# Joining the score matmuls of a tile into one planned step, with a new set of durations and priorities for a planned kernel

## The chip, the cores and the metric

The kernel runs on one core of one Trainium2 chip. The metric is the time of one execution on the device, in microseconds. Three runs of the kernel before gave 4202.29, 4206.68 and 4212.64 us; the median is 4206.68 us.

## The reference, cut to what matters

The input is sixteen sequences of 256 tokens with 128 features each, all in f32. Four blocks follow each other, and after each the sum of its input and output is normalised:

```python
x = layernorm(x + linear_attention(x))     # 4 heads of 32
x = layernorm(x + experts(x))              # 8 experts, 2 chosen, one shared
x = layernorm(x + feature_attention(x))    # 16 heads of 64, causal, softmax features
x = layernorm(x + stack(x))                # six layers
```

The six-layer stack holds the code whose matmuls are joined. Each layer is

```python
x = attention(shift_tokens(x)) + x   # 16 heads of 64, window of 32 and the 32 keys before it
x = feed_forward(shift_tokens(x)) + x   # layernorm, 128 -> 2 x 341, a * gelu(gate), 341 -> 128
```

In the attention, queries and keys are brought to length one, scaled, rotated, and multiplied for each head and each window of 32 queries with 64 keys. A masked softmax over those 64 keys weighs the values.

## The kernel before, in words

The kernel has two stages, and each has its own planner (`class Plan`). A stage is written as a set of steps. A step has an engine (`pe` is TensorE, `act` ScalarE, `dve` VectorE, `pool` GpSimd, `sp` the queue that starts DMAs), an assumed duration in us, a Python function that emits its instructions, the steps it must follow, the buffers that it takes or uses, and a rank. `Plan.run` goes through an assumed time on the host: whenever an engine is free, it takes from the ready steps the one of the lowest rank whose buffers are free, calls its function, and so writes the instructions down in that order. After a step's assumed duration and a lag per engine (`LAG`) its followers become ready. What comes out is a fixed order per engine; on the chip each engine runs its list in order and waits on semaphores. So durations, lags and ranks cost nothing by themselves on the chip: they only choose the order and the buffers. The ranks come from the position of the work (tile number), a table `due`, and the dictionary given to `Plan`, which adds a number to all steps of one function.

The first stage (the front) runs the three blocks ahead of the stack for eight units of two sequences. Its steps are `linear`, `experts`, `causal` and `part`.

The second stage runs six layers of eight units, 48 units in all. For each sequence, and in it for each tile of 128 tokens (two per sequence):

- `projections` (matmuls L1091) makes queries and keys in a `pair` buffer of PSUM; there are four `pair` buffers for the whole stage. L1112 squares them, L1098 and L1105 multiply with the rotary tables, L1115 adds, L1118 sums the squares.
- `turned` transposes them (L1165) and L1171 copies them out to `qT` and `kT`.
- `attention`: `scores` (L1239) multiplies queries and keys in small tiles, 64 rows by 32 columns, 64 matmuls per tile of tokens, into one `pair` buffer. `mask` (L1247) adds the mask, `top` (L1261) takes maxima, `exps` (L1273) exponentiates, `total` and `divide` (L1280, L1284) normalise, `turn` (L1288) transposes 32x32 blocks, and `mix` (L1298, tiles of 32 rows by 128 columns) multiplies with the inputs into two `pair` buffers, which L1307 copies out.
- `output` (L1346) applies the joined value and output weights for a sequence; `windows` (L1215) transposes its input.
- `feed_forward` does a unit of two sequences: L1372, L249, then six matmul steps `inner` (L1407) with gelu (L1414) and gating (L1420), and `outer` (L1427).

In the kernel before, `scores` is four steps per tile, each of 16 matmuls, one after the other:

```python
for g in range(4):
    sc.append(step("pe", 0.38, partial(scores, g), [..., *sc[-1:]],
                   [] if g else [pS], ..., rank + due["scores"], count=64))
```

The `pair` buffer is taken by the first of them and held until the mask has read the last. `count` is the number of instructions that the step issues on TensorE: an f32 matmul is two weight loads and two matmul records, so 16 matmuls are 64. The planner uses it in `_dense`, which holds back a step with a count over 32 as long as it and the steps before it would bring more than `BLOCK` = 256 counted instructions within `SPAN` = 3.6 us of assumed time.

Of the kernel before, what the change touches and what calls it, by code (L numbers as in the profile page):

```python
# [48 lines left out]
class Step:  # L49


    def __init__(self, eng, work, fn, after, takes, uses, rank, table, count):
        self.eng, self.work, self.fn, self.rank = eng, work, fn, rank
        self.count = count
        self.takes, self.uses, self.table = takes, uses, table
        self.next, self.wait = [], 0
        for b in (*takes, *uses):
            b.left += 1
        for s in after:
            s.next.append(self)  # L60
            self.wait += 1


class Plan:
# [6 lines left out]
    BLOCK, SPAN = 256, 3.6  # L71
# [7 lines left out]
    def step(self, eng, work, fn, after=(), takes=(), uses=(), rank=0, table=None, count=0):  # L79
# [3 lines left out]
        s = Step(eng, work, fn, after, takes, uses, rank, table, count)  # L83
# [3 lines left out]
    def run(self):  # L87
# [10 lines left out]
        now, table, opened = 0.0, None, {}  # L98
        past = []
        left = len(self.steps)  # L100
        self.log = []
        self.unique = 0
        while left:
            moved = True
            while moved:
                moved = False
                for eng, heap in ready.items():
                    if at[eng] > now or not heap:
                        continue
                    back, got, kept = [], None, ()  # L110
                    while heap and len(back) < 64:
                        item = heapq.heappop(heap)
                        s = item[2]
                        if s.table and opened and s.table not in opened:
                            back.append(item)
                            continue
                        if s.count > 32 and self._dense(s, now, past, events):
                            back.append(item)
                            continue
                        kinds = [b.kind for b in s.takes]  # L120
                        if all(self._fits(kinds, k) for k in set(kinds)) and not any(k in kept for k in kinds):
                            got = s
# [8 lines left out]
                        back.append(item)  # L131
                    for item in back:
# [5 lines left out]
                    work = got.work  # L138
                    if got.table:
# [15 lines left out]
                    if got.count:  # L155
                        past.append((now, got.count))
                        del past[:-40]
# [18 lines left out]

    def _dense(self, s, now, past, events):

        room = self.BLOCK - s.count
        for t, c in reversed(past):  # L180
            room -= c
            if room < 0:
                wait = t + self.SPAN - s.work
                if wait > now + 1e-6:
                    self.unique -= 1
                    heapq.heappush(events, (wait, self.unique, None))
                    return True
                return False
        return False
# [10 lines left out]
def tile_kernel(ctx: ExitStack, tc: tile.TileContext, a: dict, out: bass.AP):  # L200
# [84 lines left out]
    def join(step, kinds, i, lay, after, rank):  # L285
# [45 lines left out]
        for g in range(2):  # L331
            b, v, pt, pz = (Buf(k) for k in kinds)
            ld = step("sp", 2.0, partial(fetch, g, b), after, [b], [], rank)
            tn = step("pe", 0.59, partial(turn, b, pt), [ld], [pt], [b], rank, count=8)
            cp = step("act", 0.59, partial(turned_out, v, pt), [tn], [v], [pt], rank)
            pm = step("pe", 1.09, partial(product, b, v, pz), [cp], [pz], [b, v], rank, count=32)
            lay.joined.append(step("act", 0.97, partial(put, g, pz), [pm], [], [pz], rank))
# [10 lines left out]
    with ExitStack() as st:  # L348
# [5 lines left out]
        def several(pl, n, shape, name):  # L354
# [17 lines left out]
            "part.turn": 1.5,  # L372
            "experts.gated": -4,
            "experts.outer": -0.5,
            "part.divide": -2,
            "part.diagonal": -6,
            "linear.peak": -0.5,
            "experts.hidden": 1.5,
            "part.values": 1.5,
            "part.ratio": -3,  # L380
            "experts.inner": 1.0,
            "part.below": -2,
            "experts.gates": -3.0,
            "part.weigh": 2,
            "experts.turn": -4.5,
            "linear.turn": 2,
            "linear.result": 3,
            "linear.context": -2,
            "norm.stats": 1.5,
            "causal.final": 3,  # L390
            "join.product": 3,
            "part.product": -4,
            "linear.feature": -1.5,
        })
        due = {
# [57 lines left out]
        def norm(name, get, put, after, takes, uses, rank):  # L453
# [24 lines left out]
            s1 = step("dve", 2.0, stats, after, [], uses, rank)  # L478
            s2 = step("pool", 1.05, root, [s1], rank=rank)
            return step("dve", 1.4, normal, [s2], takes, uses, rank)  # L480
# [8 lines left out]
        def linear(u, before):  # L489
# [15 lines left out]
            t1 = step("pe", 0.5, partial(turn, xn, pt), [n1], [pt], [xn], rank, count=8)  # L505
# [4 lines left out]
            af = step("act", 0.78, affine, [t1, wla], [xnT], [pt], rank)  # L510
# [4 lines left out]
            kk = step("pe", 0.9, partial(feature, 1, pk), [af], [pk], [xnT], rank, count=4)  # L515
# [7 lines left out]
            mk = step("dve", 0.7, peak, [kk], [], [pk], rank)  # L523
# [10 lines left out]
            ex = step("act", 1.35, exps, [mk], [ek], [pk], rank, ("exp", 0))  # L534
            qq = step("pe", 0.9, partial(feature, 0, pq), [af], [pq], [xnT], rank, count=4)
            qc = copied(qT, None, pq, 512, [qq], [qT], [], rank, 0.59)
# [8 lines left out]
            vv = step("pe", 0.92, values, [af], [pv], [xnT], rank, count=16)  # L545
            vc = copied(v4, None, pv, 512, [vv], [v4], [], rank, 0.59)
            t2 = step("pe", 0.5, partial(turn, ek, pz), [ex], [pz], [ek], rank, count=8)
# [1136 lines left out]
```

## Time and profile before

| what | value |
| --- | --- |
| median of three runs | 4206.68 us |
| span of the profiled execution | 4210.5 us |
| busy share: TensorE, VectorE, ScalarE, GpSimd | 95%, 83%, 75%, 64% |
| granted TensorE clock, mean | 0.989 |
| second stage: from its first projection to the end | 1097.5 to 4210.5 us |
| one unit of it, from one output step to the next but one | 62.76 us (2068.36 to 2131.12) |
| TensorE's instruction records | 43728 matmuls, 43728 weight loads |

The profiled execution's own time stands beside the runs as its span, 4210.5 us: 3.8 us above the median, and inside what the three runs cover. "Busy" counts the time in which an engine has an instruction in it. Matmuls are pipelined, and an end in the profile is modelled, so what one step costs TensorE is read from the start of its first record to the start of the next step's first record. PE is TensorE's matmuls, PEld its weight loads, DVE VectorE, ACT ScalarE, POOL GpSimd.

### The profile page before, as it was taken

Reading aid. Unit: us, or ns where it says so; the run is one execution under the profiler, and the core shown is the slowest. Engines: PE = TensorE matmul, PEld = TensorE weight load, DVE = VectorE, ACT = ScalarE, POOL = GpSimd, SP = SyncE. Lnnn points to the kernel's source line nnn. Section 1 sums busy time; section 2 is a strip of 40 time slices with the busy share of each in tenths; the row PEclk is TensorE's granted clock in tenths of the full one; section 3 lists DMA queues with packets and bytes.
Section 4 is the critical chain, followed back from the end, with each engine's and each line's share of the span. In section 5 each row is a group of like instructions: output and inputs, shape, how many; then the busy total and the mean of one; then the engine's idle time right before and its main releaser. Section 6 shows DMA issues by size and latency. Waiting matters only on the chain.

```text
span 4210.5 us, 104604 instructions
## 1 busy us (share of the span) xinstructions
PE 4018.2 (95%) x43728; PEld 2659.0 (63%) x43728; DVE 3500.1 (83%) x5169; ACT 3177.9 (75%) x6138; POOL 2695.5 (64%) x2881
## 2 busy tenths in 40 slices
PE   8999999999789999999999999999999999999998
PEld 6777877877545565565565565565565565565555
DVE  6888888877688888888888888888888888888885
ACT  6666666675477887877887877887887877888885
POOL 2555455555567676676677677676767667767762
PEclk9999999999899999999999999999999999999999
DMA  3000000000000000000000000000000000000000
GB/s 91 4 6 4 6 1 4 4 4 3 20 2 2 12 13 2 7 12 2 13 2 7 12 2 13 2 7 12 2 13 2 7 12 2 2 2 7 9 12 19
DMA packets 30836, 37.03 MB, mean 9 GB/s; under 512 B 5406, under 2 KB 24348, under 8 KB 29596
## 3 DMA queue, kind: packets, MB, share of 16 engines
q1 hardware_dynamic: 30364, 30.35, 2.4%
q8 instruction: 343, 5.62, 0.6%
q14 instruction: 129, 1.06, 0.1%
HBM read 26.15 MB, written 4.19 MB: 7 GB/s over the span
## 4 chain that ended last, share of the span: by engine, by line
PE 41%; DVE 32%; ACT 12%; POOL 11%; issue 4%; SPq 0%; DMA 0%; ACTq 0%; POOLq 0%; DVEq 0%
DVE d_t L1105 8%; PE pp L1346 7%; DVE d_t L1098 7%; ACT d_sq L1112 5%; PE pp L1091 4%; PE pp L1165 3%; PE pp L1298 3%; ACT d_e L1273 3%; PE pp L1427 3%; DVE d_ss L1118 3%; POOL d_t L1115 3%; DVE d_eT L1288 2%; DVE d_e L1247 2%; PE pb L665 2%; DVE d_m L1261 2%
## 5 line engine op out<-in xcount | busy, mean ns | idle before, releaser
L1115 POOL TENSOR_TENSOR d_t<-d_t,d_t 128x1024 f32<-128x1024 f32 x384 | 905.7, 2364 | 483.6 <-DVE d_t L1098 444.2
L1273 ACT ACTIVATE d_e<-d_e,d_m,d_ny 128x64 f32<-128x64 f32 x3072 | 1063.6, 431 | 18.4 <-POOL d_m L1269 17.7
L1091 PE MATMUL pp<-d_wqkv,xs 128*128 128x512 f32 x1536 | 740.6, 611 | 19.6 <-ACT d_qT L1171 6.1
L1346 PE MATMUL pp<-d_zT,d_wvo 128*128 128x256 f32 x3072 | 684.6, 381 | 0.4 <-ACT d_qT L1171 0.2
L1346 PEld LDWEIGHTS pp<-d_zT,d_wvo 128*128 128x128 f32 x3072 | 577.5, 190 | 81.7 <-issue 2.4
L1112 ACT ACTIVATE d_sq<-pp 128x1024 f32<-128x1024 f32 x384 | 392.2, 1023 | 277.9 <-DVE d_t L1105 138.6
L1105 DVE TENSOR_TENSOR d_t<-pp,d_tab 128x1024 f32<-128x1024 f32 x384 | 467.2, 1217 | 121.2 <-ACT d_sq L1112 69.5
L1307 ACT COPY d_zT<-pp 128x1024 f32<-128x1024 f32 x384 | 369.3, 1012 | 231.2 <-PE pp L1298 231.2
L1098 DVE TENSOR_TENSOR d_t<-pp,d_tab 128x1024 f32<-128x1024 f32 x384 | 464.7, 1210 | 66.4 <-ACT d_sq L1112 64.4
L1284 POOL TENSOR_TENSOR d_e<-d_e,d_z 128x1024 f32<-128x1024 f32 x192 | 365.4, 1903 | 208.7 <-DVE d_z L1281 204.2
L1091 PEld LDWEIGHTS pp<-d_wqkv,xs 128*128 128x128 f32 x1536 | 276.0, 192 | 326.3 <-issue 239.6
L1118 DVE TENSOR_REDUCE d_ss<-d_sq 128x16 f32<-128x1024 f32 x384 | 461.6, 1202 | 7.8 <-ACT d_sq L1112 4.7
L1239 PEld LDWEIGHTS pp<-d_kT,d_qT 64*32 64x32 f32 x24576 | 234.2, 106 | 358.7 <-issue 307.8
L1165 PE MATMUL pp<-ident,d_t 128*128 128x128 f32 x3072 | 403.6, 277 | 36.3 <-ACT d_qT L1171 13.1
L1165 PEld LDWEIGHTS pp<-ident,d_t 128*128 128x128 f32 x3072 | 338.4, 142 | 151.8 <-POOL d_t L1161 49.1
L1298 PE MATMUL pp<-d_eT,d_xw 32*128 32x512 f32 x3072 | 408.3, 617 | 7.2 <-DVE d_e L1247 2.9
L855 POOL TENSOR_TENSOR c_e<-c_e,c_sm 128x1024 f32<-128x1024 f32 x128 | 248.7, 1950 | 178.2 <-DVE c_sm L851 125.0
L1161 POOL TENSOR_TENSOR d_t<-d_t,d_ny 128x1024 f32<-128x1024 f32 x192 | 361.5, 1903 | 0.0
L1407 PE MATMUL pp<-f_xn,d_w 128*128 128x512 f32 (+1 forms) x576 | 306.7, 622 | 49.5 <-ACT d_sq L1112 32.2
L1239 PE MATMUL pp<-d_kT,d_qT 64*32 64x64 f32 x24576 | 338.2, 223 | 6.6 <-issue 3.9
L1288 DVE STREAM_TRANSPOSE d_eT<-d_e 128x1024 f32<-128x1024 f32 x192 | 238.4, 1242 | 113.4 <-POOL d_e L1284 112.1
L1280 DVE TENSOR_REDUCE d_z<-d_e 128x16 f32<-128x1024 f32 x192 | 232.9, 1213 | 62.9 <-ACT d_e L1273 62.5
(186 smaller groups left out, 7176.3 us busy)
## 6 DMA issues: line engine op xcount, KB each, us to landing
d_wqkv<-L_ffn_Wqkv SPq DMA_DIRECT2D x6, 1024.0 KB
d_t<-L_ffn_Wqkv SPq DMA_DIRECT2D x10, 256.0 KB
d_t<-L_ffn_Wo SPq DMA_DIRECT2D x10, 256.0 KB, 3.4
a_xin<-L_attn_x SPq DMA_DIRECT2D x8, 256.0 KB, 2.8
keep<-bc_x SPq DMA_DIRECT2D x8, 256.0 KB, 2.0
d_t<-keep SPq DMA_DIRECT2D x8, 256.0 KB, 2.9
out<-d_t SPq DMA_DIRECT2D x8, 256.0 KB, 2.3
d_w<-L_ffn_W SPq DMA_DIRECT2D x6, 341.0 KB
```

The costliest lines, as they stand in the source:

```text
L1091: pe.matmul(pj.t[:, hf * 512 : (hf + 1) * 512], lhsT=xj, rhs=q.w["qkv"][:, c : c + 512], start=True, stop=True,)
L1098: dve.tensor_tensor(t1.t, heads(pj.t), bc(q.lay.tab[:, 0, t, cc], hs, 1), ALU.mult)
L1105: dve.tensor_tensor(t2.t.rearrange("p h (x d) -> p h x d", x=2), swapped(pj.t), bc(q.lay.tab[:, 1, t, cc].rearrange("p (x d) -> p x d", x= ...
L1112: act.activation(sq.t, heads(pj.t), AF.Square)
L1115: pool.tensor_tensor(t1.t, t1.t, t2.t, ALU.add)
L1118: dve.tensor_reduce(q.ss.t[:, t, qk, :], sq.t, AX.X, ALU.add)
L1165: pe.transpose(pz.t[:, c * P : (c + 1) * P], t1.t[:, 2 * c : 2 * c + 2, :].rearrange("p h d -> p (h d)"), ident,)
L1239: pe.matmul(pS.t[b * WIN : (b + 1) * WIN, s0 : s0 + 2 * WIN], lhsT=qT.t[r, c, b * WIN : (b + 1) * WIN], rhs=kT.t[r, c, k0 : k0 + 2 * WIN], ...
L1273: act.activation(each()[:, h, :], each()[:, h, :], AF.Exp, bias=o.m[:, h : h + 1], scale=norm_of(h),)
L1298: pe.matmul(ps[b // 2].t[:, (b % 2) * 512 : (b % 2 + 1) * 512], lhsT=q.xw.t[r, 2 * t + j, :], rhs=eT.t[r, j, :, :].rearrange("p h n -> p ( ...
L1307: act.copy(q.zT.t[:, b : b + 2, :, :].rearrange("p b h n -> p (b h n)"), pz.t)
L1346: pe.matmul(pr.t[:, :SEQ], lhsT=q.w["vo"][:, (h % 2) * 8 + h // 2, :], rhs=q.zT.t[:, :, h, :], start=(h == 0), stop=(h == HEADS - 1),)
```

## The change

The four score steps of a tile become one step of 64 matmuls, with an assumed duration of 1.07 us. `count`, `_dense`, `BLOCK` and `SPAN` are taken out. A step may have a `mode` instead; the score steps have the mode "scores" and the mix steps "mix", all others none. The planner adds `TURN` = 0.165 us of assumed time where TensorE's next step has another mode than the one before. With `STICK` = 1 (second stage only) it prefers a ready step of the mode at hand over one with another mode, if its rank is at most 1 higher. Nearly all assumed durations are set anew, mostly lower; so are the lags, and both dictionaries of priorities now name every step function, DMA steps included. The instructions of the steps themselves, the buffers and the work are the same.

```diff
-    BLOCK, SPAN = 256, 3.6
+    TURN, STICK = 0.165, 0.0
...
-                        if s.count > 32 and self._dense(s, now, past, events):
+                        if other and (s.rank > other[0] + self.STICK or s.mode != shape):
                             back.append(item)
+                            if s.rank > other[0] + self.STICK:
+                                break
                             continue
...
+                            if eng == "pe" and s.mode != shape and self.STICK and not other:
+                                other = item
+                                continue
...
+                    if eng == "pe" and got.mode != shape:
+                        work += self.TURN
+                        shape = got.mode
...
-    def _dense(self, s, now, past, events):
...
         plan = Plan(slots, {
-            "part.turn": 1.5,
-            "experts.gated": -4,
...
+            "tile_kernel.fetch_x": 9,
+            "tile_kernel.weights": 9,
...
         })
+        plan.LAG = {"pe": 0.16, "act": 0.2, "dve": 0.13, "pool": 0.61, "sp": 0.82}
...
         plan = Plan(slots, {
-            "projections.product": -9,
-            "attention.mix": -0.5,
...
+            "projections.product": -8.5,
+            "attention.scores": 2,
+            "attention.mix": -1,
+            "attention.put": -11,
...
         })
-        plan.LAG = {"pe": 0.27, "act": 0.2, "dve": 0.25, "pool": 0.2, "sp": 2.5}
+        plan.LAG = {"pe": 0.17, "act": 0.06, "dve": 0.02, "pool": 0.64, "sp": 3.08}
+        plan.STICK = 1
...
-                    "pe", 1.82, partial(product, qk, pj), [*q.ready, *q.loaded, q.gate(t)],
-                    [pj, t1], rank=rank + due["project"], count=8,
+                    "pe", 1.76, partial(product, qk, pj), [*q.ready, *q.loaded, q.gate(t)],
+                    [pj, t1], rank=rank + due["project"],
...
-            def scores(g):
-
-                for c in (2 * g, 2 * g + 1):
+            def scores():
+
+                for c in range(8):
                     for par in range(2):
...
-            sc = []
-            for g in range(4):
-                sc.append(
-                    step(
-                        "pe", 0.38, partial(scores, g), [o.done[0], *q.turned[: t + 1], *sc[-1:]],
-                        [] if g else [pS], [qT, kT] + ([pS] if g else []), rank + due["scores"],
-                        count=64,
-                    )
-                )
-            mk = step("dve", 1.19, mask, sc, [e], [pS], rank + due["mask"])
+            sc = [
+                step(
+                    "pe", 1.07, scores, [o.done[0], *q.turned[: t + 1]], [pS], [qT, kT],
+                    rank + due["scores"], mode="scores",
+                )
+            ]
+            mk = step("dve", 1.13, mask, sc, [e], [pS], rank + due["mask"])
...
-                "pe", 2.05, partial(mix, ps), [te, q.spread, *q.mixed], [*ps, *new],
-                [eT, q.xw] + ([] if new else [q.zT]), rank + due["mix"], count=32,
+                "pe", 1.93, partial(mix, ps), [te, q.spread, *q.mixed], [*ps, *new],
+                [eT, q.xw] + ([] if new else [q.zT]), rank + due["mix"], mode="mix",
```

The order that the planner now writes for a unit in the middle of the second stage can be read from the program without running it. TensorE has four score steps per unit, each as 64 matmuls in a row, and right behind each of them a mix step of another tile. The six `inner` steps stand together behind the third pair of these, apart from one projection after the first of them. In the whole program there are 191 places where TensorE comes to score matmuls from something else, where there were 637.

## The prediction

> **What bounds the kernel now.** I read the page first: shares of busy time, the queues, then the timeline of a unit in the middle of the second stage, and last the two places where TensorE stands still in the midst of score matmuls.
>
> ```profile
> PE 4018.2 (95%) x43728; PEld 2659.0 (63%) x43728; DVE 3500.1 (83%) x5169; ACT 3177.9 (75%) x6138; POOL 2695.5 (64%) x2881
> q8 instruction: 343, 5.62, 0.6%
> PE 41%; DVE 32%; ACT 12%; POOL 11%; issue 4%; SPq 0%; DMA 0%; ACTq 0%; POOLq 0%; DVEq 0%
> ```
>
> TensorE is the bound, with VectorE next. The second line is the fetching of instructions (packets, MB, share of the DMA engines): 343 packets for 2 x 43728 TensorE records, that is one packet of 16 KB for about 255 of them. Next, the windows view over one unit, and the timeline inside it:
>
> ```profile
> 2068.36:2131.12 62.76, 61.03 (x773) 37.09 (x772) 54.48 (x66) 50.76 (x97) 43.97 (x50) 1.00 0.06 20
> ```
>
> ```profile
> 2089.72 0.45 PE L1239 MATMUL pp<-d_kT,d_qT 64*32 64x64 f32 x32
> 2090.10 1.12 PE L1407 MATMUL pp<-f_xn,d_w 128*128 128x512 f32 x2
> 2091.16 0.45 PE L1239 MATMUL pp<-d_kT,d_qT 64*32 64x64 f32 x32
> 2091.54 1.12 PE L1407 MATMUL pp<-f_xn,d_w 128*128 128x512 f32 x2
> 2092.59 0.45 PE L1239 MATMUL pp<-d_kT,d_qT 64*32 64x64 f32 x32
> 2093.93 1.09 PE L1407 MATMUL pp<-f_xn,d_w 128*85 128x512 f32 x2 [0.88 <-ACT d_sq L1112]
> 2094.95 0.45 PE L1239 MATMUL pp<-d_kT,d_qT 64*32 64x64 f32 x32
> 2095.33 2.00 PE L1298 MATMUL pp<-d_eT,d_xw 32*128 32x512 f32 x16
> ```
>
> Order of the window's columns: length, then busy us of PE, PEld, DVE, ACT, POOL, clock, DMA share, GB/s. PE has work in 61.03 of 62.76 us at full clock, but "busy" hides loss: a group of 16 score matmuls costs 0.38 (start to next start), and an L1407 that is followed by one costs 1.05 (2090.10 to 2091.16) where it costs 0.86 before other work. This score tile holds one of the four PSUM buffers from 2089.72 to 2095.33.
>
> The unit counted step by step, at the shortest start-to-start of each kind: 8 projections x 1.72, 8 transposes x 0.87, 2 windows x 0.44, 4 mixes x 1.93, 2 outputs x 6.91, 6 inner x 0.86, outer 2.68, two turns x 0.44: 51.9 us. Scores: 13 single groups x 0.385 and one run of three, 1.20: 6.2. What the step ahead of a score group lasts longer, 14 times, from 0.06 (mix) and 0.09 (projection) to 0.19 (L1346, 7.10 for 6.91): 2.0 together, mean 0.143. That is 60.1; the other 2.6 us are waits, the largest 0.95, 0.67 and 0.58 us.
>
> **Scores joined.** In the fill of the stage four groups stand in one run:
>
> ```profile
> 1246.40 1.49 PE L1239 MATMUL pp<-d_kT,d_qT 64*32 64x64 f32 x128
> 1247.81 1.13 PE L1298 MATMUL pp<-d_eT,d_xw 32*128 32x512 f32 x4
> ```
>
> 64 matmuls take 1.42 us to the next start, and that is the new step with the new follower, a mix. Four per unit are 5.7 for 6.2: 0.52 x 48 units = 25 us saved. Entries fall from 637 to 191 by the two programs' orders: 446 x 0.143 = 64 us. All of it lies on TensorE, the path. Together **-89 us**.
>
> **The guard taken out.** `_dense` kept 256 counted instructions from following each other within 3.6 us. What it guarded against shows where its accounting failed:
>
> ```profile
> 1278.22 2.53 PE L1239 MATMUL pp<-d_kT,d_qT 64*32 64x64 f32 x219 [0.32 <-DVE d_t L1098]
> 1282.72 0.31 PE L1239 MATMUL pp<-d_kT,d_qT 64*32 64x64 f32 x5 [1.97 <-issue]
> ```
>
> Two tiles' scores ran at full rate and then TensorE stopped for 1.97 us with nothing to wait for but issue. An instruction packet starts at 1280.08; the next score matmul starts 2.6 us after that. A second stop, 1.14 us at 1159.37, has a packet at 1157.00, 2.4 us ahead. My reading: the packet for the page after next is asked for when a page of 256 begins, and a page that runs out sooner than that packet is usable stops TensorE. From the beginning of the page (256 instructions before the last one that ran) to the resumption I count 3.4 us at the first stop and 3.1 at the second; pages of the steady stage that lasted 3.16 to 3.20 us end without a stop. I take 3.2.
>
> A joined step is 256 instructions, a page in length; its fastest 256 take 1.1 to 1.3 us. It is hit only where its place in the pages is nearly aligned, so that fewer than some 20 instructions of other work (about 9 per us) fall into the same page. A unit has 1540 instructions plus a few waits, six pages and a little, so the place drifts slowly and comes by every offset. Laying the program's TensorE instructions into pages of 256, each priced as above, gives 37 pages of 343 below 3.2 us, short of it by 37.5 us in sum (31 us at 3.0, 45 at 3.4). The same count on the kernel before gives 12 pages and 5.6 us. So **+32 us** (26 to 40); below nothing is excluded, since more dense pages cannot ask for fewer packets.
>
> The Trainium skill ("Runtime: NRT & Kernel Launch", Instruction fetch mechanics) says that the next 16 KiB page is fetched while the present one runs, and that crossing a boundary is mostly hidden. By that sentence the 32 would be 0 and the forecast 4056; the stop of 1.97 us above speaks against it for score matmuls, and I go by the row.
>
> **Waits in the second stage.** Of the 2.6 us per unit the largest are before L1407 and transposes: they wait for ScalarE or VectorE to hand back a PSUM buffer.
>
> ```profile
> PE pp L1407 <- ACT d_sq L1112: 32.2, 38, 0.9
> PE pp L1407 <- DVE d_t L1098: 17.0, 35, 0.6
> PE pp L1165 <- ACT d_qT L1171: 13.1, 41, 0.3
> ```
>
> In that unit scores hold a buffer while still being computed for 3.6, 5.6, 11.6 and 3.8 us, 24.6 of the 251 buffer-us that four buffers have; joined, 4 x 1.42 = 5.7. That frees 19 buffer-us, 7.5%. The interleaving of L1407 with scores, which makes the 0.95 us wait, is gone in the new order: the six stand together, two gates behind a projection's 1.72 us. On the other side a mix now stands right behind each score step, so that three of four buffers are needed at once, and VectorE must keep up with a shorter unit: 54.48 us of work in some 60 instead of 62.76. Bounds: all 2.6 us gone (125 us), or none. The new waits take the place of some old ones; I take half, **-62 us**, having no row nearer to one end.
>
> **Other edits.** Durations, lags and ranks cost nothing themselves. The front has no joined step; its order changes throughout. TensorE idles there for about 61 of the first 1100 us by the windows view; I take 0, bounds 30 either way (half of that idle time). SP's DMAs keep their kinds and count; those for the first input and weights stand in the same order. A layer's weights are fetched into the other of two sets while a layer of some 500 us runs, which covers them; were it gone, 1 MB at the 256 KB rows' 2.0 to 3.4 us would be 8 to 14 us for each of five layers. ScalarE's table loads are 159 against 158 by the two orders.
>
> **Sum.** 4210.5 - 89 + 32 - 62 + 0 = 4091.5 of span. The median of the runs is 3.8 below that span: **4088 us**.
>
> **Rivals.** (1) Only the joined scores count, and the waits stay as long as they were: 4210.5 - 89 + 32 - 3.8 = 4150. For it: VectorE and ScalarE chains are unchanged. Against: the buffers freed. (2) All waits go: 4025. For it: the new orders have a regular unit, and every feed-forward wait found above belongs to the old interleaving. (3) VectorE takes over: its 8.3 idle us per unit stay, for its order waits for ScalarE and GpSimd as before, and nothing is gained: 4207. For it: 32% of the chain. Against: TensorE's own sum explains 60 of 62.76. (4) The slower end: instruction fetch takes over. If nearly every joined step is stopped, not only aligned ones, by the mean of the two stops seen, 1.55 us, that is 192 x 1.55 = 298, less the 5 already there: 4210.5 - 89 - 62 + 293 - 3.8 = 4349. It decides from a mean of 0.8 us per joined step ((89 + 62) / 192); I count 0.2. For it: a joined step is a page long. Against: the run at 1246.40 ends without a stop, and in between lie 129 slow instructions per tile.
>
> **How the numbers follow.** Forecast 0.50 (4040 to 4140), rival 1 0.22, rival 2 0.10, rival 3 0.06, rival 4 0.12. About 0.3%, 13 us, is what a measurement of this kernel can tell from no change. Rival 3 is mostly within that (0.05, the rest faster); rival 4 is slower: 0.12; all others faster: 0.83. The range goes down to rival 2 with half of the front's possible gain, 4010, and up to rival 1 with the front's loss and the larger fetch sum, 4190; outside lie rivals 3 and 4, some 0.18.
>
> **What would show it.** Right: score records in runs of 128, 1.42 us to the next start; steady unit at 59 to 61 us; some tens of stops of 0.5 to 2 us in L1302 put down to issue, with an instruction packet in each. Wrong: a unit of 62 us with new idle time before L1361 or L1228 (rivals 1, 3); stops in most score steps (4); a front that ends more than 30 us from 1097.

## The result, and the profile after

The changed kernel takes 4360.15 us (median of four runs, 4356.45 to 4366.18) against 4208.68 us for the kernel before (four runs, 4202.29 to 4212.64). The ratio is 1.0363, 95% interval 1.0348 to 1.0377: 151 us slower, where 119 us less than the median of the first three runs had been forecast. The profiled execution has a span of 4357.5 us.

The page of the changed kernel, the lines that answer to those shown of before:

```profile
PE 4039.2 (93%) x43728; PEld 2733.0 (63%) x43728; DVE 3503.9 (80%) x5169; ACT 3173.1 (73%) x6139; POOL 2699.3 (62%) x2881
q8 instruction: 343, 5.62, 0.5%
DVE 40%; PE 33%; ACT 13%; POOL 8%; issue 5%; DMA 0%; SPq 0%; ACTq 0%; DVEq 0%; POOLq 0%
```

VectorE, ScalarE and GpSimd have the same busy time as before, within 0.2%, in a longer span. The chain of waits has turned over: VectorE 40% and TensorE 33%, where it was 32% and 41%. The mean granted clock of TensorE fell from 0.989 to 0.980.

From here on the line numbers are those of the changed kernel: `projections` L1154, its readers `first` L1161, `second` L1168, `square` L1175 (before: L1091, L1098, L1105, L1112), the sum over the squares L1181, turning L1228, put L1234, `scores` L1302, `mix` L1361, `output` L1406, `inner` L1467. In experiments that add lines to the kernel, they are a few higher.

The unit that stands in the place of the one shown before (length, busy us of PE, PEld, DVE, ACT, POOL, clock, DMA share, GB/s), and the timeline of TensorE within it:

```profile
2069.16:2134.49 65.33, 61.72 (x772) 39.26 (x770) 54.53 (x66) 50.43 (x96) 44.18 (x51) 0.97 0.01 2
```

```profile
2082.04 1.49 PE L1302 MATMUL pp<-d_kT,d_qT 64*32 64x64 f32 x128
2083.46 1.13 PE L1361 MATMUL pp<-d_eT,d_xw 32*128 32x512 f32 x4
2084.96 1.99 PE L1361 MATMUL pp<-d_eT,d_xw 32*128 32x512 f32 x12 [0.37 <-DVE d_t L1168]
2088.54 1.33 PE L1228 MATMUL pp<-ident,d_t 128*128 128x128 f32 x8 [1.59 <-DVE d_t L1168]
2089.66 8.64 PE L1406 MATMUL pp<-d_zT,d_wvo 128*128 128x256 f32 x32
2098.14 1.88 PE L1154 MATMUL pp<-d_wqkv,xs 128*128 128x512 f32 x4
```

The joined score step does what was said of it: 128 records in one run and 1.42 us to the mix behind it (2082.04 to 2083.46). But the unit is 65.33 us long, not 62.76. The mix shown costs 5.08 us to the next step (2083.46 to 2088.54), where it needs 1.93: it stops in its middle and again behind it, both times for `second` on VectorE. The `output` step then takes 8.48 us to the next start where it took 6.91. The windows view over the stop behind the mix and over `output` says why:

```profile
2087.00:2088.50 1.50, 0.00 (x0) 0.00 (x0) 1.25 (x2) 1.50 (x6) 0.40 (x1) 1.00 0.00 0
2088.50:2092.50 4.00, 3.96 (x15) 3.23 (x16) 3.96 (x5) 4.00 (x7) 2.58 (x2) 0.59 0.00 0
2092.50:2096.00 3.50, 3.50 (x18) 3.09 (x17) 3.00 (x3) 1.60 (x6) 3.10 (x6) 0.98 0.00 0
```

The clock column reads 1.00, 0.59, 0.98: after the stop TensorE is granted half its clock for 3.41 us. Such spells (clock 0.5 in the rows of the trace) take 92 us between 1250 and 4000 us of the changed kernel, 27 of them, and none of the kernel before in the same stretch, which is called the steady part from here on; in the whole run 176 and 96 us. What VectorE and ScalarE did in those microseconds:

```profile
2081.25 1.21 DVE L1161 TENSOR_TENSOR d_t<-pp,d_tab 128x1024 f32<-128x1024 f32 x1
2083.68 1.23 DVE L1168 TENSOR_TENSOR d_t<-pp,d_tab 128x1024 f32<-128x1024 f32 x1 [1.22 <-ACT d_sq L1175]
2084.82 1.22 DVE L1161 TENSOR_TENSOR d_t<-pp,d_tab 128x1024 f32<-128x1024 f32 x1
2087.26 1.23 DVE L1168 TENSOR_TENSOR d_t<-pp,d_tab 128x1024 f32<-128x1024 f32 x1 [1.22 <-ACT d_sq L1175]
```

```profile
2082.55 1.02 ACT L1175 ACTIVATE d_sq<-pp 128x1024 f32<-128x1024 f32 x1 [0.66 <-DVE d_t L1161]
2086.13 1.02 ACT L1175 ACTIVATE d_sq<-pp 128x1024 f32<-128x1024 f32 x1 [1.23 <-DVE d_t L1161]
```

One projection's PSUM buffer has three readers: `first` and `second` on VectorE, `square` on ScalarE. Here they run first, square, second, one behind the other, and VectorE stands still for 1.22 us, twice in 3.6 us, while ScalarE squares. The planner has no edge between them and counts them as free to run side by side. In the traces the square never overlaps either of the others: in none of 526 pairs of neighbouring readers of one buffer (a square and a reader on VectorE) before, in none of 620 after. The Trainium skill ("PSUM — Partial Sum Buffer", section on bank collisions) states that two engines may not be in one bank and quadrant of PSUM at once, reads against reads included, and that the scheduler of the compiler back end adds a dependency between any two instructions on different engines that touch the same one; both traces agree with it, by their 0 overlaps. The waits of VectorE, first of the kernel after, then of the kernel before:

```profile
DVE d_t L1168 <- ACT d_sq L1175: 141.5, 143, 2.1
DVE d_t L1161 <- ACT d_sq L1175: 60.1, 56, 1.7
DVE d_ss L1181 <- ACT d_sq L1175: 51.8, 44, 1.4
```

```profile
DVE d_t L1105 <- ACT d_sq L1112: 69.5, 59, 6.7
DVE d_t L1098 <- ACT d_sq L1112: 64.4, 53, 3.9
```

Columns: us in total, times, longest. The square stands between the two in 236 of 384 buffers after (141 second-square-first, 95 first-square-second); before it stood between them in 142, all of them second-square-first. VectorE's idle time that the square ends, gaps under 0.15 us included, went from 143 to 254 us. TensorE's own waits are now led by one for `second`, and one of the front comes next:

```profile
PE pp L1228 <- DVE d_t L1168: 75.1, 47, 2.0
PE pb L913 <- DVE c_e L897: 45.6, 49, 1.9
PE pp L1302 <- DVE d_t L1161: 29.6, 35, 1.2
PE pp L1228 <- POOL d_t L1224: 28.7, 43, 6.7
```

By stage: the second stage begins at 1155.9 us instead of 1097.5 (+58) and lasts, up to TensorE's last matmul, 3192.0 us instead of 3104.1 (+88). TensorE's second stage can also be counted step by step: each step's start to the next step's start, less the shortest such time of its kind (the same for all kernels: 1.93 us for a mix, 1.42 for a joined score step), is "excess". It was 311 us before and is 419 after, 108 more, while the steps themselves got 20 us shorter; the largest part, 165 us, stands between a mix and a turn.

### The profile page after: what moved, and what is told of

It is laid out like the page before. It is cut to its first block, busy times and chain, and to the rows that moved or that the text cites. A ratio compares the mean times of both kernels' runs of the same rounds, so it can differ in the third digit from the quotient of the medians.

```text
span 4357.5 us, 104680 instructions
## 1 busy us (share of the span) xinstructions
PE 4039.2 (93%) x43728; PEld 2733.0 (63%) x43728; DVE 3503.9 (80%) x5169; ACT 3173.1 (73%) x6139; POOL 2699.3 (62%) x2881
## 3 DMA queue, kind: packets, MB, share of 16 engines
q14 instruction: 131, 1.07, 0.1%
## 4 chain that ended last, share of the span: by engine, by line
DVE 40%; PE 33%; ACT 13%; POOL 8%; issue 5%; DMA 0%; SPq 0%; ACTq 0%; DVEq 0%; POOLq 0%
PE pp L1406 9%; DVE d_t L1168 8%; ACT d_sq L1175 6%; DVE d_t L1161 6%; PE pp L1154 5%; PE pp L1228 4%; DVE d_ss L1181 3%; DVE d_eT L1351 3%; DVE c_e L897 2%; POOL d_e L1347 2%; PE pb L913 2%; ACT d_e L1336 2%; DVE f_h L1480 2%; DVE d_z L1343 2%; DVE c_sm L889 2%
## 5 line engine op out<-in xcount | busy, mean ns | idle before, releaser
L1154 PE MATMUL pp<-d_wqkv,xs 128*128 128x512 f32 x1536 | 721.6, 603 | 9.6 <-DVE d_t L1161 5.9
L1406 PE MATMUL pp<-d_zT,d_wvo 128*128 128x256 f32 x3072 | 718.3, 394 | 1.1 <-ACT d_zT L1370 0.5
L1406 PEld LDWEIGHTS pp<-d_zT,d_wvo 128*128 128x128 f32 x3072 | 607.3, 199 | 115.5 <-issue 22.2
L1175 ACT ACTIVATE d_sq<-pp 128x1024 f32<-128x1024 f32 x384 | 392.6, 1022 | 339.7 <-DVE d_t L1161 160.2
L1168 DVE TENSOR_TENSOR d_t<-pp,d_tab 128x1024 f32<-128x1024 f32 x384 | 465.8, 1214 | 205.4 <-ACT d_sq L1175 141.5
L1228 PEld LDWEIGHTS pp<-ident,d_t 128*128 128x128 f32 x3072 | 351.7, 145 | 296.4 <-DVE d_t L1168 113.4
L1228 PE MATMUL pp<-ident,d_t 128*128 128x128 f32 x3072 | 416.5, 283 | 126.8 <-DVE d_t L1168 75.1
L1161 DVE TENSOR_TENSOR d_t<-pp,d_tab 128x1024 f32<-128x1024 f32 x384 | 462.7, 1205 | 60.1 <-ACT d_sq L1175 60.1
L1181 DVE TENSOR_REDUCE d_ss<-d_sq 128x16 f32<-128x1024 f32 x384 | 463.1, 1206 | 51.9 <-ACT d_sq L1175 51.8
L1361 PE MATMUL pp<-d_eT,d_xw 32*128 32x512 f32 x3072 | 447.5, 623 | 27.2 <-DVE d_t L1168 17.1
L1154 PEld LDWEIGHTS pp<-d_wqkv,xs 128*128 128x128 f32 x1536 | 274.8, 191 | 288.7 <-issue 218.4
L1302 PEld LDWEIGHTS pp<-d_kT,d_qT 64*32 64x32 f32 x24576 | 254.9, 105 | 150.3 <-DVE d_t L1161 66.9
L1302 PE MATMUL pp<-d_kT,d_qT 64*32 64x64 f32 x24576 | 285.9, 226 | 32.8 <-DVE d_t L1161 29.6
L881 POOL TENSOR_TENSOR c_e<-c_mn,c_e 128x512 f32<-128x512 f32 x128 | 136.3, 1065 | 265.6 <-DVE c_mn L878 200.9
L1467 PE MATMUL pp<-f_xn,d_w 128*128 128x512 f32 (+1 forms) x576 | 270.6, 600 | 6.7 <-ACT f_h L1474 3.3
```

The costliest lines, as they stand in the source:

```text
L1154: pe.matmul(pj.t[:, hf * 512 : (hf + 1) * 512], lhsT=xj, rhs=q.w["qkv"][:, c : c + 512], start=True, stop=True,)
L1161: dve.tensor_tensor(t1.t, heads(pj.t), bc(q.lay.tab[:, 0, t, cc], hs, 1), ALU.mult)
L1168: dve.tensor_tensor(t2.t.rearrange("p h (x d) -> p h x d", x=2), swapped(pj.t), bc(q.lay.tab[:, 1, t, cc].rearrange("p (x d) -> p x d", x= ...
L1175: act.activation(sq.t, heads(pj.t), AF.Square)
L1181: dve.tensor_reduce(q.ss.t[:, t, qk, :], sq.t, AX.X, ALU.add)
L1228: pe.transpose(pz.t[:, c * P : (c + 1) * P], t1.t[:, 2 * c : 2 * c + 2, :].rearrange("p h d -> p (h d)"), ident,)
```

## Experiments

Each experiment is timed against the kernel before on its own chip, whose median lay between 4206.84 and 4213.5 us.

**Which part of the change costs.** The first four planned anew.

`e1_join_only`: the kernel before with the score steps joined, its durations and priorities kept.

```diff
-            sc = []
-            for g in range(4):
-                sc.append(step("pe", 0.38, partial(scores, g), ..., count=64))
+            sc = [step("pe", 1.52, scores, [o.done[0], *q.turned[: t + 1]], [pS], [qT, kT],
+                       rank + due["scores"])]
```

> The kernel before with the score steps of a tile joined (one step of assumed 1.52 us, the guard idle), all its other durations, lags and priorities kept. Theory A (the new stage-two order is at fault: it sets the square between the two VectorE readers of a projection's PSUM buffer, so that VectorE idles, buffers come back late, TensorE waits and its clock halves): the join alone is faster than before, 4100 to 4180 us, with no half-clock spells in the steady stage. Theory B (the join itself is at fault, because a score step with a mix behind it wants three of four PSUM buffers at once): slower than before by the 89 us of stage two, about 4295 us. Theory C (instruction fetch): above 4250 us, with stops put down to issue in or behind the score runs.

Measured 4426.73 us, ratio 1.0518 (1.0497 to 1.0539). Theories A and B fail by their numbers. The time lies in theory C's range, but its mechanism is absent: stops of TensorE over 0.4 us put down to issue sum to 5.3 us. Excess is 538 us, VectorE's idle time ended by the square 299 us, half clock in the steady part 48 us.

`e2_four_steps`: the changed kernel with four score steps again.

```diff
-            sc = [step("pe", 1.07, scores, ..., mode="scores")]
+            for g in range(4):
+                sc.append(step("pe", 0.27, partial(scores, g), ..., mode="scores"))
```

> The changed kernel with its new durations, lags and priorities, but four score steps of 16 matmuls again (assumed 0.27 us each, mode kept, no guard). Theory A: the order at fault stays, so 4340 to 4450 us. Theory B: the 89 us of stage two come back, about 4270 us. Theory C: as B or lower, if the steps are spread out again.

Measured 4521.28 us, ratio 1.0749 (1.0726 to 1.0773): the new priorities do not fit four steps either.

`e3_old_front`: the changed kernel with the front of before: its durations, lags and priorities.

```diff
-            "tile_kernel.fetch_x": 9,
-            "tile_kernel.weights": 9,
...
+            "part.turn": 1.5,
+            "experts.gated": -4,
...
```

> The front of the kernel before (its order), stage two of the changed kernel. Stage two begins 58 us later in the changed kernel than before (1155.9 for 1097.5 us). If the front's order costs that by itself: 4302 us, within 8. Rival: part of the late begin is made good at the seam, since stage two then finds its weights and units ready: 4320 to 4345 us.

Measured 4292.74 us, ratio 1.0200 (1.0185 to 1.0216). The front's new order costs 67 us; the second stage lasts about as long as in the changed kernel (3186.9 us up to the last matmul).

`e4_chain`: edges square, second, first added to the steps of the changed kernel, so that the planner knows that they exclude each other.

```diff
+                a2 = step("dve", 1.13, partial(second, qk, pj, t2), [s, q.tabbed], ...)
+                a1 = step("dve", 1.13, partial(first, qk, pj, t1), [a2, q.tabbed], ...)
```

> The changed kernel with two more edges in its second plan: square, then second, then first of a projection, so that the planner knows that the three readers of one buffer follow each other on the chip. Theory A: VectorE's idle time ended by the square falls from 254 us to below 100, TensorE's half-clock spells of the steady stage go, and the time falls to 4280 us or less. Theories B and C: within 25 us of 4360.

Measured 4524.41 us, ratio 1.0747 (1.0712 to 1.0783): not the fall that theory A forecast. VectorE's idle time ended by the square rose to 338 us, half clock took 171 us. The edges made the planner draw all orders anew, on every engine, so it does not isolate the order of three readers; nor do e1 and e2 isolate the join. From here on most experiments keep the planned order and move single steps behind the planner.

**One step moved on one engine.** `e5_square_behind`: in the changed kernel's finished order, a square that stands between the two VectorE readers of its buffer goes behind the second of them, if that is still ahead of the sum which needs it.

```diff
...
+        for s in order:
+            if s.pair:
+                lo, hi = sorted(place[r] for r in s.pair)
+                if lo < place[s] < hi < place[s.sums]:
+                    place[s] = hi + 0.5
+        for s in sorted(order, key=place.get):
+            s.fn()
...
```

> The changed kernel; where ScalarE's square is written between the two VectorE readers of the same PSUM buffer, it is written behind both instead. TensorE's, VectorE's and GpSimd's orders are the same, ScalarE's alone differs. Theory A (VectorE waits for the square in the midst of a projection, hands the buffer back late, and TensorE waits for it behind a mix): VectorE's idle time ended by the square falls from 254 us to below 150, the 165 us that TensorE loses between a mix and the transposes behind it fall to below 80, and the time to 4230 to 4290 us. Rival D (VectorE has too much to do ahead of that place in any order of the readers): 4335 to 4385 us.

Measured 4291.27 us, ratio 1.0194 (1.0178 to 1.0209), against 1.0363 for the changed kernel: 69 us gained with TensorE's, VectorE's and GpSimd's orders untouched. All 236 squares that stood between the readers now follow both; 126 of them change their place in ScalarE's own list, and for the others only who waits for whom is turned round. The half clock in the steady part is gone (92 to 0 us), and mix to turn fell from 165 to 122 us. The secondary numbers that were expected for the waits did not come: VectorE's idle time ended by the square fell to 216 us only (below 150 expected), the 122 us are not below 80, and TensorE now waits for the square.

```profile
PE pp L1372 <- ACT d_sq L1185: 45.0, 90, 1.1
PE pp L1239 <- ACT d_sq L1185: 33.3, 84, 2.8
```

(L1372 is the mix there, L1239 the turn, L1185 the square.) It is many short waits, 174 of them with 0.45 us in the mean, where the turn's line for `second` had 47 with 1.6 us, and no half clock follows them in the steady part. Of the 69 us up to 46 are clock (92 us at half speed), the rest waits. The buffers are not handed back sooner: from the start of a projection to the end of its last reader it is 7.0 us in the mean, 6.9 in the changed kernel (steady part, the kernel's steps matched to the records). What the move changed is how long the single waits are.

`e6_old_front_square_behind`: the edits of e3 and e5 together.

> The same in the version with the front of the kernel before (4293 us). Theory A: 4160 to 4225 us, 67 us below the run beside it. Rival D: 4270 to 4320 us.

Measured 4226.84 us, ratio 1.0043 (1.0028 to 1.0057). The old front and the moved squares together take back all but some 16 of the 151 us. The move is a repair and not the order of before, in which 142 squares stood between the readers too.

`e7_before_square_behind`: the lines of e5 in the planner of the kernel before.

> The same in the kernel before, where 142 of 384 squares stand between the two readers. Theory A, if it bounds that kernel too: 4130 to 4190 us. If its VectorE has slack at those places: within 15 us of 4207.

Measured 4272.24 us, ratio 1.0149 (1.0133 to 1.0166): here it costs 61 us, neither of the two forecasts, and the excess from a mix to the scores behind it rises from 17 to 74 us. So "the square behind both" is no rule. Which of the three should be last depends on which TensorE step waits for what they make next; that reason is read from the two traces, not tested by itself.

`e8_nudge`: the kernel before with the mix's assumed duration set from 2.05 to 2.00 us.

```diff
-                "pe", 2.05, partial(mix, ps), [te, q.spread, *q.mixed], [*ps, *new],
+                "pe", 2.00, partial(mix, ps), [te, q.spread, *q.mixed], [*ps, *new],
```

> The kernel before with one assumed duration changed, the mix step's 2.05 to 2.00 us; nothing else. Theory E (the planner's order is a chance draw around the durations, and the priorities of the kernel before are fitted to just this draw): over 1% off, and rather slower, 4250 to 4400 us. Rival: within 15 us of 4207, and then the join's 220 us with old priorities must have a cause of its own.

Measured 4217.29 us, ratio 1.0010 (1.0001 to 1.0020). So this new plan is no loss to speak of. But it is one draw, and a near one: 93 of TensorE's 3924 steps change place. That a plan drawn wholly anew, as in e1, can lose by chance is not excluded by it.

**The join alone, all else in the order of before.** `e9_join_at_first`: score steps 2 to 4 go right behind the first; every other step keeps its place.

```diff
...
+        for s in order:
+            for k, g in enumerate(s.four or ()):
+                place[g] = place[s] + 0.1 * k
...
```

> The kernel before, its plan made as it was, with the guard; only then are the second to fourth score step of a tile written right behind its first. All other steps keep their order on every engine. If the join by itself pays as the prediction's sum has it (fewer entries, shorter runs): 4110 to 4175 us, and score runs of 128 records at 1.42 us. Theory B (a run of scores in one piece makes other steps wait): 4200 us or more. Theory C (fetch): stops put down to issue, over 30 us in sum.

Measured 4204.95 us, ratio 0.9991 (0.9981 to 1.0002): 7 us less, which is not to be told from nothing. The unit and a part of TensorE's timeline in it:

```profile
2068.08:2130.63 62.55, 60.00 (x773) 37.43 (x771) 54.83 (x66) 50.65 (x97) 43.98 (x50) 1.00 0.06 21
```

```profile
2078.65 2.00 PE L1306 MATMUL pp<-d_eT,d_xw 32*128 32x512 f32 x16
2081.84 1.07 PE L1173 MATMUL pp<-ident,d_t 128*128 128x128 f32 x8 [1.19 <-ACT d_zT L1315]
2091.13 1.98 PE L1416 MATMUL pp<-f_xn,d_w 128*128 128x512 f32 x4
2093.84 1.09 PE L1416 MATMUL pp<-f_xn,d_w 128*85 128x512 f32 x2 [0.72 <-ACT d_sq L1120]
```

TensorE is busy 1.03 us less than in the unit before (60.00 to 61.03), but the unit is only 0.21 us shorter. In it stand waits of 1.19 and 0.72 us for ScalarE, which empties PSUM buffers there; the first is new, and it recurs:

```profile
PE pp L1173 <- ACT d_zT L1315: 41.7, 35, 1.2
```

Over the second stage the score matmuls cost 20 us less, and what the step ahead of them lasts longer fell by some 62 us (637 entries to 190, by the median of each kind of step), 82 us together. The stage got 8 us shorter, so some 74 us came back as waits, the most ahead of turns (excess there 68 us before, 136 here) and of projections (44 and 62).

`e10_join_at_last`: steps 1 to 3 go right ahead of the fourth instead.

```diff
-                place[g] = place[s] + 0.1 * k
+                place[g] = place[s.four[3]] - 0.1 * (3 - k)
```

> As the run beside it, with the first three score steps of a tile written right ahead of its fourth instead. Entries are saved alike; the PSUM buffer is written late, not read earlier or later. If the join pays by itself in any place: 4110 to 4190 us, at most 25 us from the run beside it. Theory B: 4200 us or more.

Measured 4314.85 us, ratio 1.0244 (1.0226 to 1.0263), with 89 us of half clock. The scores now begin later than before and end as late, and the gaps ahead of them stay empty: excess between one `inner` step and the next is 99 us. So no run with joined scores was faster than the 4205 us of e9; whether some other order lets the whole join pay is not shown.

**Which part of the plan.** `e11_front_new_ranks`: e3 with the changed kernel's front priorities; only the front's durations and lags are those of before.

```diff
-            "part.turn": 1.5,
...
+            "tile_kernel.fetch_x": 9,
+            "tile_kernel.weights": 9,
...
```

> The changed kernel with the front's durations and lags of before but the front's new priorities. If the priorities cost the front its 67 us: 4340 to 4380 us. If the new durations and lags do: 4285 to 4305 us, as with the whole old front.

Measured 4350.77 us, ratio 1.0333 (1.0317 to 1.0348): the new priorities alone bring back 58 of the 67 us that the new front costs, which leaves 9 for durations and lags.

`e12_stack_old_ranks`: the changed kernel with the second stage's priorities of before.

```diff
-            "projections.product": -8.5,
-            "attention.scores": 2,
...
+            "projections.product": -9,
+            "attention.mix": -0.5,
...
```

> The changed kernel with the second stage's priorities of before; its joined steps, new durations, lags and modes stay. If the new priorities are at fault in stage two: 4270 to 4320 us, nearer to before plus the front's 67. If the old ones only fit the old durations and the four steps: 4380 to 4500 us, as the join alone with old priorities and durations was (4427).

Measured 4442.90 us, ratio 1.0548 (1.0530 to 1.0567). With joined scores the old priorities are worse than the new by 83 us.

**Is TensorE the bound?** Three kernels in the order of before leave work of one engine out.

`e13_half_output`: half of the matmuls of the `output` product.

```diff
-                for h in range(HEADS):
+                for h in range(HEADS // 2):
...
```

> The kernel before, its order kept; each output product does 8 of its 16 matmuls (half of the heads are left out), 3.45 us less of TensorE for each of 96, 331 us in all. If TensorE bounds stage two, as the prediction had it: 3870 to 3920 us. If a loop through VectorE, ScalarE and the PSUM buffers does: less than a third of that comes back, 4100 us or more.

Measured 4303.95 us, ratio 1.0219 (1.0202 to 1.0236): with 331 us of TensorE's work gone the kernel is 90 us *slower*. Its page and its waits (line numbers of the kernel before: L1298 the mix, L1165 the turn):

```profile
PE 3909.3 (91%) x42192; PEld 2451.1 (57%) x42192; DVE 3500.3 (81%) x5169; ACT 3178.0 (74%) x6138; POOL 2696.5 (63%) x2881
```

```profile
PE pp L1298 <- ACT f_xn L1401: 56.0, 40, 1.4
PE pp L1165 <- DVE xs L1355: 54.0, 40, 1.5
PE pp L1298 <- DVE xs L1355: 47.3, 44, 1.9
```

TensorE's busy time fell by 109 us only, for the clock was halved in 37 spells (253 us of the steady part; mean over the run 0.952). By mean clock times span, 206 us are lost to the clock here and 46 in the kernel before; without that difference of 160 us the run would have been some 70 us faster than before, by my estimate, of 331 taken out. The run itself can't separate the two: it shows that the work is not missed one for one, and not how much of it was on the path.

`e14_half_reduce`: VectorE's sum over the squares takes half of the features; TensorE's work is untouched.

```diff
-                dve.tensor_reduce(q.ss.t[:, t, qk, :], sq.t, AX.X, ALU.add)
+                dve.tensor_reduce(q.ss.t[:, t, qk, :], sq.t[:, :, : DH // 2], AX.X, ALU.add)
```

> The kernel before, its order kept; VectorE's sum of the squares reads half of each head's features, about 0.5 us less for each of 384, some 200 us of VectorE in all. If TensorE bounds: within 30 us of 4207. If the loop through VectorE does: 4060 to 4140 us.

Measured 4175.82 us, ratio 0.9913 (0.9897 to 0.9928): 38 us less, between the two forecasts. This sum reads `sq` in SBUF and no PSUM buffer, so the run tests VectorE's load and not the readers of the buffer.

`e15_half_square`: ScalarE's square, too, covers half of them.

```diff
-                act.activation(sq.t, heads(pj.t), AF.Square)
+                act.activation(sq.t[:, :, : DH // 2], heads(pj.t)[:, :, : DH // 2], AF.Square)
...
```

> As the run beside it, and ScalarE's square too is of half of each head's features, some 0.4 us less for each of 384 and the PSUM buffer read for so much shorter. If the buffer's three readers one behind the other are the loop: another 60 to 150 us below the run beside it. If TensorE bounds: within 30 us of it.

Measured 4108.52 us, ratio 0.9753 (0.9739 to 0.9768). The excess on TensorE falls from 311 to 208 us, though nothing of TensorE's was changed:

```profile
PE 3988.2 (97%) x43728; PEld 2644.7 (64%) x43728; DVE 3314.5 (81%) x5169; ACT 3015.4 (73%) x6138; POOL 2693.8 (66%) x2881
```

The last 67 us come with 159 us less of ScalarE, the first 38 with 185 us less of VectorE. The shorter square also reads its buffer for less time (1.02 to 0.60 us); whether that or ScalarE's load brought the 67 us, the run does not separate.

**A version that beats both.** `e16_pairs`: the order of before, with score step 2 right behind 1, and 4 right behind 3.

```diff
...
+                place[s.four[1]] = place[s.four[0]] + 0.1
+                place[s.four[3]] = place[s.four[2]] + 0.1
...
```

> The kernel before, its plan made as it was; only then the second score step of a tile is written right behind the first, and the fourth right behind the third. Half of the join's saving on TensorE, some 45 us. If the waits that the whole join raised come from the four steps no longer filling gaps: 4165 to 4195 us, faster than before and than the whole join (4205). If TensorE's savings come back as waits whatever is saved: 4200 to 4215 us.

Measured 4192.16 us, ratio 0.9951 (0.9935 to 0.9968): 21 us faster than the kernel before. Entries fall from 637 to 366, and two pieces of TensorE work per tile are left to fill gaps. Excess is 282 us, 29 less than before.

## Why the prediction was wrong, by its steps

**"Scores joined", -89 us.** The size on TensorE was about right (82 us counted in e9) and the step behind it, "All of it lies on TensorE, the path", failed. e9 has just this edit, and gives -7 us where -89 was due: some 74 us came back as waits, the most ahead of turns. My evidence for the bound was 61.03 busy us of 62.76. That shows that TensorE is full, not that what fills it is needed: "busy" includes fillers such as the single score groups between `inner` steps, which run while a buffer is being emptied. e13 takes out 331 us of TensorE's work and loses; e14 and e15 take out none of it and win 38 and 105 us. So work of VectorE and ScalarE is on the path as well. That the loop which sets the unit goes through the four `pair` buffers (a projection fills one, three readers that exclude each other empty it at 1.2 + 1.2 + 1.0 us, and TensorE may fill it again) is my reading and not shown: only e15 shortens a reader, another number of buffers was not tried, and all four buffers are in use for only some 31% of the steady part before and 33% after. Rival 3 had the right engine ("its 8.3 idle us per unit stay"), but priced it at no change.

**"Waits in the second stage", -62 us.** Wrong in sign: excess rose by 108 us, and both of my bounds lay at zero or below. What I had argued from did come: excess ahead of an `inner` step fell from 62 to 13 us. But ahead of a turn it rose from 68 to 214. The buffer time that the join was to free was freed and used up again: a score tile's hold on its buffer, from its first matmul to the end of the mask, fell from 8.6 to 4.9 us in the mean, from 13.6% to 7.6% of the four buffers' time in the steady part, but projections, mixes, turns and `inner` steps hold theirs longer, and the four are held for 74% of the time in both kernels. I wrote that "three of four buffers are needed at once" and gave it no price. The row that had one was in the profile: VectorE's wait for the square, 69.5 and 64.4 us before, was put aside since VectorE was not the bound. In the changed order it stands where projections, scores and a mix come close together, and e5 shows that the place of the square alone is worth 69 us there.

**What was not in the sum: the clock.** Full clock in the steady stage was taken for granted. With the stops behind the mix came 92 us of half clock, up to 46 us of time, and in e13 253 us. The Trainium skill ("TensorE: Matmul & The Clock Gate", Part 1) puts the penalty for ramping the clock at under 1% of a typical span. Here the whole run's 176 us at half clock are some 88 us, 2% of the span. Its windows of about 3.4 us agree with the 3.41 us of the spells.

**"Other edits", 0 for the front.** It cost 67 us (e3), twice my bound of 30. e11 puts 58 of that on the priorities. I had taken the bound from TensorE's idle time of before, which limits a gain and not a loss. The waits that are new there are TensorE's transposes for VectorE's clamp (45.6 us in 49 waits at L913, against 8.0 before) and GpSimd's for VectorE (25.7 us before; all idle time of GpSimd ahead of that line, whoever ended it, grew from 200 to 266 us):

```profile
POOL c_e L881 <- DVE c_mn L878: 200.9, 30, 17.0
```

Which of these costs the time was not tried.

**"The guard taken out", +32 us.** It cost about 1. All stops of TensorE over 0.4 us put down to issue sum to 4.5 us after and 3.9 before, and of the 192 joined score steps one has such a stop. The others run through, as this one:

```profile
1983.62 1.49 PE L1302 MATMUL pp<-d_kT,d_qT 64*32 64x64 f32 x128 [0.28 <-DVE f_h L1480]
1985.04 2.36 PE L1361 MATMUL pp<-d_eT,d_xw 32*128 32x512 f32 x14
```

These 256 instructions ran out in 1.4 us, far below my 3.2, without a stop. So a short page is not sufficient, and the step that failed is "a page that runs out sooner than that packet is usable stops TensorE". Nor is every such stop one of a short page: ahead of the 1.9 us at a turn, the last 256 instructions had taken 30 us. My reading, which no run tests, is that the fetch has a lead where slow matmuls stand ahead. In the stop of 1.97 us that I argued from, TensorE had worked off a run of 219 score records right behind a wait. The rule of the skill that I had set against my row, that crossing a page is mostly hidden, was the better one here.

**Rival 4**, 4349 us, lies within 11 us of the result, but its mechanism is absent: 1.9 us of stops at a single turn, 1.8 at a score step, where 293 were needed. A right number is no evidence for its cause.

**What stays open.** Some 16 us of e6 over the kernel before. Why e1, the joined steps planned with the old priorities, costs 220 us: VectorE's waits for the square grew to 299 us there too, but all engines' orders differ and nothing was isolated. And what in e7's order makes the same move of the square a loss.

## What to carry to other kernels

A bound engine is shown by taking work from it, and from the engines beside it, not by its busy share: ask of each busy interval whether someone waits for it, or whether it fills a gap. Work that fills a gap can be worth nothing when removed (e9), and less than nothing when the idle time that is left halves the clock (e13), so read the clock of such a run first. Where a planner chooses the order, look in its plan for steps that exclude each other on the chip, such as two engines that read one PSUM buffer, and test the plan by moving single steps in the finished order rather than by planning anew, which changes everything at once: told of the exclusion by edges and left to plan again, the planner here came out slower (e4). Try to pair short steps before joining them all: here half the join won 21 us, the whole join in the same order nothing that can be measured.

## What the runs showed of the hardware

- Readers of one PSUM buffer on VectorE and ScalarE ran strictly one behind the other (0 overlaps in 1146 neighbouring pairs); a square of 1.02 us cost VectorE 1.22 us of idle time where it came between the two in VectorE's list.
- A stop of 1.6 us on an otherwise 94% busy TensorE was followed by 3.41 us at half clock, in which an `output` step took 8.48 instead of 6.91 us. The longest stop ahead of each of the 27 such spells of the changed kernel's steady part was 1.58 to 1.94 us; but not every such stop is followed by one: the stop of 1.97 us at 1282.72 in the kernel before was not.
- A shorter product can make a kernel slower: 331 us less of matmuls, 90 us more of time (e13).
- 256 TensorE instructions ran out in 1.4 us without a stop for issue, in all but one of the changed kernel's 192 joined score steps.
